# A decoder layer on one core: the next group's first norm is made inside this group's scan, in the buffer of the sums within chunks

## The chip, the core and the metric

The kernel runs on one core of a Trainium2 chip. The metric is device time in microseconds (us), the median of several executions. One more execution was recorded by the hardware profiler; every duration of a single instruction below comes from that execution, whose own time is told apart from the median.

The engines are named as the profile names them: PE multiplies matrices (and transposes, by a product with a unit matrix), PEld loads its weights, DVE works on vectors, ACT applies functions and copies, POOL is the general engine, SP issues most of the transfers. Each runs its own list of instructions in order, and they meet in semaphores.

## What is computed

One decoder layer over 64 sequences of 128 tokens with 256 features, all in float32. In short:

```
xn = layernorm(x) * gamma + beta                  # the first norm
x_inner, z = split(xn @ W_in)                     # 256 -> 2 x 512
xc = silu(conv4(x_inner) + b)                     # causal, 4 taps, per channel
B, C, delta = split(xc @ W_x)                     # 16, 16, 1
y = selective_scan(xc, A, B, C, softplus(delta))  # h = exp(dt*A)*h + dt*B*x ; y = C.h
x1 = layernorm(x + x + ((y + xc * D) * silu(z)) @ W_out)
x2 = layernorm(x1 + decayed_attention(x1, context))
out = layernorm(x2 + shared_ffn(x2) + sum of the best 2 of 8 routed ffns, weighted)
```

The scan is not run step by step. Its decay is the same for all channels, so it becomes products: within a sequence of 128 tokens, pairs of tokens in different chunks of 16 are coupled by a product of `cj` and `bj` on PE, pairs in the same chunk by elementwise sums (the "sums within chunks", tile `eq`), and both together make the 128 x 128 matrix `mt` that multiplies the scaled inputs `xd`.

## The kernel before, in words

The 64 sequences are 16 groups of 4. Each group goes through a first half (`front`, L632, then `scan`, L750), a second half (`after`, L824: output projection, norm, attention, norm; then `route`, L946: router, ranks, scatter of the rows to a buffer in DRAM) and a shared feed-forward network (`early_shared`, L1069). After 4, 8, 12 and 16 groups a batch of tiles of routed rows is listed, and the tiles' feed-forward networks (`one_tile`, L1284) run beside the later groups and, after all groups, alone. At the end the rows come back, are added, normalised and stored.

These strands are Python generators. Each `yield` says how long, in the builder's own books (`work[0]`), the strand should let others put work on PE before it goes on. `abreast` (L1312) always advances the able strand with the smallest due time, and `placed` (L1330) gives a strand its due time from the work and waits it has passed. So the order of PE's list is fixed while the program is built; after that, each of the other engines' lists is put in order by the scheduler of the framework, which may move an instruction ahead of ones that were written before it.

`first_halves` (L1500) takes group 0 and then groups 2 to 15; group 1 has a strand and buffers of its own.

The steps that the change and the prediction touch, in their order within a first half:

- `front` takes the buffer `xn` (one slot, tag "xn"), calls `layernorm` (L577) for groups other than 0, waits 2.6 in the books, transposes `xn` on PE into `xnT` (L548, L606), waits 1.2, and projects with `w_in_s`: four products with a convolution after each (L657, L662), four for the gate `sz` (L674). Then the projection with `w_x_s` and its copy `bcs` (L687), whose rows go through DRAM and come back as `bj`, `cj` and `cq` (L692 to L719, all issued by SP), a transposition of `bcs` (L695), and a chain of small operations on DVE and ACT that makes the step size `dl` (L726 to L747).
- `layernorm` issues, for 4 sequences, 4 bn_stats and 4 bn_aggr on DVE (L583, L584), an addition (L586), a power on POOL (`rstd`, L588), a product on DVE (`shift`, L590), yields 4.2 in the books, and then 4 activations on ACT that write the normalised rows (L593).
- `scan` multiplies `bj` and `cj` by masks on POOL (L754), spreads `dl` (`d1`, `dlb`, L757, L761), sums it with products (`after_in`, L764; `middle`, L773), takes the buffer `eq` under the tag "xn", which is the slot that `xn` had (L765), takes exponentials on ACT (L778, L779), multiplies `bj` and `cj` (L780, L781), multiplies `cj` by `bj` on PE (L785), and makes the sums within chunks on DVE (L788, L789, `gq` L793, then `mt` L795, L799). Then four blocks of `xc` are transposed and copied by ACT to `xd` (L806, L807), and four times four products `mt` by `xd` (L813) are combined on DVE (L817, L820).

The one slot that the change uses twice, and the wait in the books that it touches:

```
def buffer(st, shape, name, tag=None):
    if "own" not in st:
        return one.tile(shape, F32, name=name, tag=tag or name)
...
        xn = buffer(st, [P, GB, D], "xn", "xn")
...
        eq = buffer(st, [P, GB, NS, Q], "eq", "xn")
```

A new tile of a tag with one slot may be written only when the readers of the tile before it in that slot are done.

Of the kernel before, what the change touches and what calls it, by code (L numbers as in the profile page):

```python
# [16 lines left out]
P = 128  # L17
L = 128
D = 256
# [10 lines left out]
GB = 4  # L30
# [481 lines left out]
def _shared_decay(ctx, K):  # L512
    tc, nc = K.tc, K.tc.nc
    NG = K.x.shape[0] // GB
# [32 lines left out]
    def turn(out, src, ident):  # L547
        work[0] += 0.11  # L548
        nc.tensor.transpose(out, src, ident)  # L549
# [4 lines left out]
# [4 lines that stand above are left out]
        return shaped(st["own"][tag or name], shape)  # L558

    def little(st, shape, name, bufs=1):  # L560
        if "own" not in st:
            return small.tile(shape, F32, name=name, bufs=bufs)
        size = int(np.prod(shape[1:]))
        rest = st["own"]["little"]
        st["own"]["little"] = rest[:, size:]
        return shaped(rest, shape)

    def shaped(flat, shape):
        names = "abc"[: len(shape) - 1]
        sizes = dict(zip(names, shape[1:]))  # L570
        return flat[:, 0 : int(np.prod(shape[1:]))].rearrange(
            f"p ({' '.join(names)}) -> p {' '.join(names)}", **sizes
        )
# [3 lines left out]
    def layernorm(dst, src):  # L577

        n = src.shape[1]
        mv = small.tile([P, GB, 2], F32, name="mv")[:, 0:n, :]  # L580
        for b in range(n):
            st = small.tile([P, nc.vector.BN_STATS_DIM], F32, name="st")
            nc.vector.bn_stats(st, src[:, b, :])  # L583
            nc.vector.bn_aggr(mv[:, b, :], st)  # L584
        var = small.tile([P, GB], F32, name="var")[:, 0:n]
        nc.vector.tensor_scalar(var, mv[:, :, 1], EPS, None, ALU.add)  # L586
        rstd = small.tile([P, GB], F32, name="rstd")[:, 0:n]
        nc.gpsimd.tensor_tensor(rstd, var, mhalf[:, 0:n], ALU.pow)  # L588
        shift = small.tile([P, GB], F32, name="shift")[:, 0:n]
        nc.vector.scalar_tensor_tensor(shift, mv[:, :, 0], -1.0, rstd, ALU.mult, ALU.mult)  # L590
        yield 4.2
        for b in range(n):
            nc.scalar.activation(  # L593
                dst[:, b, :], src[:, b, :], AF.Identity, bias=shift[:, b : b + 1], scale=rstd[:, b : b + 1]
            )
# [14 lines left out]
    def seqs(ap):  # L610
        return ap.rearrange("p (b l) -> p b l", l=L)
# [15 lines left out]
    def load_x(g):  # L627
        xt = xts[g % 3]
        nc.gpsimd.dma_start(out=xt, in_=x[g * GB : (g + 1) * GB].rearrange("b l d -> l b d"))
        return xt  # L630

    def front(st):  # L632


        xt = st["xt"]
        xn = buffer(st, [P, GB, D], "xn", "xn")
        if st is states[0]:
            rstd, shift = K.norm0
            for b in range(GB):
                read_by = nc.scalar.activation(  # L640
                    xn[:, b, :], xt[:, b, :], AF.Identity, bias=shift[:, b : b + 1], scale=rstd[:, b : b + 1]
                )
            first_read.append(read_by.ins.name)
        else:
            yield from layernorm(xn, xt)
        yield 2.6
        xnT = buffer(st, [P, KD, T], "xnT", "xnT")
        transposed(xnT, xn, gam, bet)
        yield 1.2
# [100 lines left out]
    def scan(st):  # L750

        xcf, dl, tok, bj, cj, cq = (st[k] for k in ("xcf", "dl", "tok", "bj", "cj", "cq"))
        for t, h in ((bj, halvesT[0]), (cj, halvesT[1])):
            nc.gpsimd.tensor_tensor(seqs(t), seqs(t), h.unsqueeze(1).to_broadcast([KB, GB, L]), ALU.mult)  # L754

        d1 = little(st, [P, GB, Q], "d1")
        nc.vector.tensor_tensor(  # L757
            d1, dl.unsqueeze(2).to_broadcast([P, GB, Q]), place.unsqueeze(1).to_broadcast([P, GB, Q]), ALU.mult
        )
        dlb = little(st, [P, GB, 32], "dlb")  # L760
        nc.vector.tensor_copy(dlb, dl.unsqueeze(2).to_broadcast([P, GB, 32]))  # L761
        yield 4.4 if fetched[0] else 2.4
        pin = pm.tile([P, GB, Q], F32, name="pm")
        product(pin.rearrange("p b i -> p (b i)"), lhsT=after_in, rhs=d1.rearrange("p b i -> p (b i)"), start=True, stop=True)  # L764
        eq = buffer(st, [P, GB, NS, Q], "eq", "xn")  # L765
        nc.vector.tensor_tensor(
            eq, pin.unsqueeze(2).to_broadcast([P, GB, NS, Q]),
            a_row.unsqueeze(1).unsqueeze(3).to_broadcast([P, GB, NS, Q]), ALU.mult,
        )
        pof = pm.tile([KB, T], F32, name="pm")  # L770
        for b in range(GB):
            for q in range(4):
                product(  # L773
                    pof[32 * q : 32 * q + 32, b * L : (b + 1) * L], lhsT=dlb[:, b, :], rhs=middle[min(q, 2)],
                    start=True, stop=True, tile_position=(0, 32 * q),
                )
        eb = buffer(st, [KB, T], "eb", "bcs")
        nc.scalar.activation(eb, pof, AF.Exp, scale=a_col)  # L778
        nc.scalar.activation(eq, eq, AF.Exp)  # L779
        nc.vector.tensor_tensor(bj, bj, eb, ALU.mult)  # L780
        nc.vector.tensor_tensor(cj, cj, eb, ALU.mult)  # L781
        yield 4.2
        pmt = pm.tile([P, GB, L], F32, name="pm")
        for b in range(GB):
            product(  # L785
                pmt[:, b, :], lhsT=bj[:, b * L : (b + 1) * L], rhs=cj[:, b * L : (b + 1) * L], start=True, stop=True
            )
        nc.vector.tensor_tensor(eq, eq, cq, ALU.mult)  # L788
        nc.vector.tensor_tensor(  # L789
            eq, eq, tok[:, :, 0:NS].unsqueeze(3).to_broadcast([P, GB, NS, Q]), ALU.mult  # L790
        )
        gq = little(st, [P, GB, Q], "gq")
        nc.vector.tensor_reduce(gq, eq.rearrange("p b n i -> p b i n"), AX.X, ALU.add)  # L793
        mt = buffer(st, [P, GB, NQ, Q], "mt", "dm")
        nc.vector.tensor_tensor(  # L795
            mt, gq.unsqueeze(2).to_broadcast([P, GB, NQ, Q]), causal.unsqueeze(1).to_broadcast([P, GB, NQ, Q]), ALU.mult
        )
        mtf = mt.rearrange("p b j i -> p b (j i)")
        nc.vector.tensor_tensor(mtf, mtf, pmt, ALU.add)  # L799
        yield  # L800

        xd = [buffer(st, [P, 2, DI], f"xd{j}", tag) for j, tag in enumerate(("xnT", "xd"))]
        for b in range(GB):
            ps = pm.tile([P, DI], F32, name="pm")
            for c in range(CI):
                turn(ps[:, c * P : (c + 1) * P], xcf[:, c, b * L : (b + 1) * L], ident)  # L806
            nc.scalar.activation(xd[b // 2][:, b % 2, :], ps, AF.Copy, scale=dl[:, b : b + 1])  # L807
            yield 0.5 if b < GB - 1 else 3.6
        acc = st["sz"]
        for c in range(CI):  # L810
            ps = pm.tile([P, GB, L], F32, name="pm")
            for b in range(GB):
                product(  # L813
                    ps[:, b, :], lhsT=xd[b // 2][:, b % 2, c * P : (c + 1) * P], rhs=mtf[:, b, :], start=True, stop=True
                )
            y = xcf[:, c, :]
            nc.vector.scalar_tensor_tensor(  # L817
                y, xcf[:, c, :], dsk[:, c : c + 1], ps.rearrange("p b l -> p (b l)"), ALU.mult, ALU.add
            )
            nc.vector.tensor_tensor(acc[:, c, :], acc[:, c, :], y, ALU.mult)  # L820
            yield 0.5 if c < CI - 1 or not fetched[0] else 2.0
        st["acc"] = acc
# [507 lines left out]
    def placed(gen, at, length, span=1.0):  # L1330

        passed = 0.0
        while True:
            before = work[0]
            try:
                wait = next(gen) or 0.0
            except StopIteration:
                return
            passed += work[0] - before + wait
            yield at + span * min(1.0, passed / length), wait  # L1340
# [15 lines left out]
    states = [{} for _ in range(NG)]  # L1356
# [142 lines left out]

    def first_halves():  # L1500
        states[2]["xt"] = load_x(2)
        yield from placed(start, 0.0, 54.0)
        states[0]["scanned"] = True
        for g in range(2, NG):
            if g + 1 < NG:
                yield from until(lambda: "read" in states[g - 2], g - 1)
                states[g + 1]["xt"] = load_x(g + 1)
            yield from placed(first_half(states[g]), g - 1, 54.0)
            states[g]["scanned"] = True
# [327 lines left out]
```

## Time and profile before

| | |
|---|---|
| median of 3 executions | 1954.57 us (1946.59 to 1956.8) |
| the profiled execution, its own time | 1935.52 us |
| its span, first to last instruction | 1933.7 us |
| mean granted clock of PE | 0.988 |
| busy: PE, DVE, ACT, POOL | 97%, 50%, 39%, 24% |
| PE idle, by stretch: 0 to 80 us | 21.8 us |
| 80 to 400 us | 16.5 us |
| 400 to 1450 us | 11.2 us |
| 1450 to the end | 18.1 us |

The idle time of a stretch is its length less PE's busy time in the table of stretches. PE's busy time is counted with modelled ends, so a PE that is shown busy may still have short pauses. A row of a wait names the engine that waited, the line and tile it waited with, who released it, the total, the number of waits and the longest.

### The profile page before, as it was taken

The page shows a single profiled execution, that of the slowest core. Times are in us where ns is not written, and L with a number is a line of the kernel's source. Part 1 is how long each engine was busy: PE and PEld are TensorE (multiplying, and loading weights), DVE is VectorE, ACT ScalarE, POOL GpSimd, SP SyncE. Part 2 cuts the span into 40 slices and gives each one's busy share as a digit, 9 for nine tenths or more (in the row PEclk, how much of TensorE's full clock was granted, in tenths as well). Part 3 has the DMA queues.
Part 4 walks back from the last instruction along what each step waited for, and adds up shares of the span by engine and source line. Part 5 has one row for each costly group of instructions (what it writes and reads, how often), then busy time and mean ns, then how long its engine had stood idle before and what let it go on. Part 6 is the DMA issues. An engine that isn't in the chain of part 4 may idle for free.

```text
span 1933.7 us, 26599 instructions
## 1 busy us (share of the span) xinstructions
PE 1866.0 (97%) x9252; PEld 1393.1 (72%) x9252; DVE 971.9 (50%) x2409; ACT 748.7 (39%) x1238; POOL 473.1 (24%) x715
## 2 busy tenths in 40 slices
PE   7799999999999998999999999999999999999997
PEld 3656656668686856787877768786877888999554
DVE  5766667745455557455555474554333111111774
ACT  5553553443434343535353544352231222222233
POOL 2102212303030403132322313141313322222111
PEclk9999999999999998999999999999999999999998
DMA  4211211423150214323242224232204443353782
GB/s 142 53 35 44 68 49 41 137 85 95 45 153 28 85 35 153 101 77 113 64 133 93 79 93 123 61 123 92 81 19 128 146 150 118 120 175 107 276 305 89
DMA packets 101352, 199.10 MB, mean 103 GB/s; under 512 B 22904, under 2 KB 61432, under 8 KB 96600
## 3 DMA queue, kind: packets, MB, share of 16 engines
q1 hardware_dynamic: 80952, 144.24, 23.6%
q0 software_dynamic: 17328, 51.41, 7.8%
q10 hardware_dynamic: 2928, 1.65, 0.3%
q8 instruction: 75, 1.23, 0.3%
q14 instruction: 69, 0.57, 0.1%
HBM read 206.81 MB, written 58.08 MB: 137 GB/s over the span
## 4 chain that ended last, share of the span: by engine, by line
PE 72%; DVE 3%; issue 3%; DMA 2%; ACT 2%; POOL 2%; SPq 0%; POOLq 0%; ACTq 0%; DVEq 0%
PE pm L545 37%; PE gu L545 32%; PE pm L549 4%; DMA picked<-ys 1%; POOL rstd L588 1%; DMA ys<-rows_out,to 1%; DVE st L583 0%; DVE x L1305 0%; DMA cq<-chunks 0%; POOL xs L1028 0%; ACT x L593 0%; ACT xn L593 0%; DVE hc L1051 0%; DVE xt L1305 0%; ACT xc L667 0%
## 5 line engine op out<-in xcount | busy, mean ns | idle before, releaser
L545 PE MATMUL gu<-rows_T,routed_gu 128*128 128x256 f32 (+1 forms) x2496 | 499.4, 351 | 1.5 <-ACT rows_T L1232 1.5
L545 PEld LDWEIGHTS gu<-rows_T,routed_gu 128*128 128x128 f32 x2496 | 417.7, 191 | 59.2 <-issue 14.2
L1261 DVE TENSOR_TENSOR hid<-hid,gu 128x512 f32<-128x512 f32 x135 | 92.7, 687 | 394.8 <-PE gu L545 344.4
L545 PE MATMUL pm<-routed_d,hid 128*128 128x256 f32 x1080 | 252.7, 381 | 0.0
L545 PE MATMUL gu<-x2T,shared_w 128*128 128x512 f32 x512 | 232.0, 596 | 4.4 <-DVE hc L1051 3.3
L545 PE MATMUL pm<-xnT,w_in_s 128*128 128x512 f32 x480 | 226.6, 599 | 1.7 <-ACT xnT L606 1.1
L545 PEld LDWEIGHTS pm<-routed_d,hid 128*128 128x128 f32 x1080 | 199.7, 190 | 29.6 <-issue 5.4
L1277 POOL DMA_INDIRECT ys<-rows_out,to x135 | 135.0, 1000 | 331.4 <-ACT rows_out L1276 282.8
L545 PEld LDWEIGHTS gu<-x2T,shared_w 128*128 128x128 f32 x512 | 94.3, 190 | 112.1 <-issue 93.6
L593 ACT ACTIVATE x<-x,shift,rstd 128x256 f32<-128x256 f32 x156 | 82.3, 590 | 232.5 <-DVE shift L590 222.2
L588 POOL TENSOR_TENSOR rstd<-var,mhalf 128x4 f32<-128x4 f32 (+1 forms) x69 | 72.8, 1055 | 370.6 <-DVE var L586 318.6
L662 DVE SCALAR_TENSOR_TENSOR xc<-pm,cw,xc 128x508 f32<-128x508 f32 (+1 forms) x180 | 131.4, 738 | 37.2 <-ACT xc L657 36.0
L545 PEld LDWEIGHTS pm<-xnT,w_in_s 128*128 128x128 f32 x480 | 90.2, 192 | 80.3 <-issue 72.3
L1276 ACT ACTIVATE rows_out<-pm,wt 128x256 f32<-128x256 f32 x135 | 57.9, 471 | 205.2 <-PE pm L545 185.4
L1260 ACT ACTIVATE hid<-gu 128x512 f32<-128x512 f32 x135 | 80.6, 597 | 110.0 <-PE gu L545 109.7
L545 PE MATMUL pm<-w_out_s,sz 128*128 128x256 f32 x512 | 116.4, 381 | 0.4 <-ACT xd L807 0.2
L545 PEld LDWEIGHTS pm<-w_out_s,sz 128*128 128x128 f32 x512 | 95.4, 191 | 14.3 <-issue 1.0
L657 ACT ACTIVATE xc<-pm,cb,cw 128x512 f32<-128x512 f32 x60 | 46.7, 778 | 144.2 <-PE pm L545 144.2
L1028 POOL DMA_INDIRECT xs<-x,index x64 | 71.6, 1118 | 78.0 <-DVE row L1024 42.8
L583 DVE BATCH_NORM_STATS2 st<-x 128x6 f32<-128x256 f32 x196 | 77.4, 408 | 1.6 <-DMA x<-in_x_dram 0.7
L545 PE MATMUL gu<-shared_w,hc 128*128 128x256 f32 x320 | 72.5, 380 | 0.0
L1051 DVE TENSOR_TENSOR hc<-hc,gu 128x512 f32<-128x512 f32 x64 | 43.5, 680 | 55.2 <-PE gu L545 35.1
(288 smaller groups left out, 2571.2 us busy)
## 6 DMA issues: line engine op xcount, KB each, us to landing
routed_gu<-in_ffn_dram SPq DMA_DIRECT2D x78, 1024.0 KB
routed_d<-in_ffn_dram SPq DMA_DIRECT2D x78, 512.0 KB
picked<-ys SPq DMA_DIRECT2D x16, 1024.0 KB
rows_in<-xs SPq DMA_DIRECT2D x57, 258.0 KB
cT<-in_ctxT_dram POOLq DMA_DIRECT2D x16, 512.0 KB, 4.1
x_rows<-x SPq DMA_DIRECT2D x16, 512.0 KB
cq<-chunks SPq DMA_DIRECT2D x15, 512.0 KB
x<-in_x_dram POOLq DMA_DIRECT2D x9, 512.0 KB, 4.2
```

The costliest lines, as they stand in the source:

```text
L545: nc.tensor.matmul(out, lhsT=lhsT, rhs=rhs, **how)
L549: nc.tensor.transpose(out, src, ident)
L583: nc.vector.bn_stats(st, src[:, b, :])
L588: nc.gpsimd.tensor_tensor(rstd, var, mhalf[:, 0:n], ALU.pow)
L593: nc.scalar.activation(dst[:, b, :], src[:, b, :], AF.Identity, bias=shift[:, b : b + 1], scale=rstd[:, b : b + 1])
L657: nc.scalar.activation(xcf[:, c, :], ps, AF.Identity, bias=cb[:, c : c + 1], scale=cw[:, c, TAPS - 1 : TAPS],)
L662: nc.vector.scalar_tensor_tensor(xc[:, c, :, s:], ps3[:, :, : L - s], cw[:, c, TAPS - 1 - s : TAPS - s], xc[:, c, :, s:], ALU.mult, ALU.add,)
L1028: s = nc.gpsimd.indirect_dma_start(out=xs, in_=rows[k][:, b, :], in_offset=None, out_offset=bass.IndirectOffsetOnAxis(ap=index[:, b, k : k ...
L1260: nc.scalar.activation(hc, psg, AF.Silu)
L1261: nc.vector.tensor_tensor(hc, hc, psu, ALU.mult)
L1276: nc.scalar.activation(y[:, j, :], ps[:, j, :], AF.Copy, scale=wt[:, j : j + 1])
L1277: s = nc.gpsimd.indirect_dma_start(out=ys, in_=y[:, j, :], in_offset=None, out_offset=bass.IndirectOffsetOnAxis(ap=to[:, j : j + 1], axis=0),)
```

## The change

The scan of a group whose successor's input is there now ends its sums within chunks by taking the slot "xn" again, for the next group's `xn`, and starts the next group's `layernorm` (the part ahead of its yield). The second part, the four activations, is written after the last `xd`. The next group's `front` finds `xn` made and skips the norm and the wait of 2.6. This is so for the norms of groups 2 to 15, made in the scans of group 0 and of groups 2 to 14; groups 0 and 1 are as before.

```diff
@@ front
         xt = st["xt"]
-        xn = buffer(st, [P, GB, D], "xn", "xn")
-        if st is states[0]:
+        made = "xn" in st
+        if made:
+            xn = st["xn"]
+        else:
+            xn = buffer(st, [P, GB, D], "xn", "xn")
+        if made:
+            pass
+        elif st is states[0]:
...
         else:
             yield from layernorm(xn, xt)
-        yield 2.6
+        yield 0.0 if made else 2.6
@@ scan, after mt is made
         nc.vector.tensor_tensor(mtf, mtf, pmt, ALU.add)
+
+        norm = None
+        if "next" in st:
+            then = st["next"]
+            xn = then["xn"] = buffer(then, [P, GB, D], "xn", "xn")
+            norm = layernorm(xn, then["xt"])
+            next(norm)
         yield
@@ scan, after the last xd
+        for _ in norm or ():
+            pass
@@ first_halves
         states[2]["xt"] = load_x(2)
+        for g in (0, *range(2, NG - 1)):
+            states[g]["next"] = states[max(g + 1, 2)]
```

Lines of the kernel after the change stand 6 lower from the transposition in `front` on, 13 lower at `xd` and 15 lower behind it.

## The prediction

> **What bounds the kernel now.** First the page's head: is one engine the bound, and where does it pause?
>
> ```profile
> span 1933.7 us, 26599 instructions
> ...
> PE 1866.0 (97%) x9252; PEld 1393.1 (72%) x9252; DVE 971.9 (50%) x2409; ACT 748.7 (39%) x1238; POOL 473.1 (24%) x715
> ...
> PE   7799999999999998999999999999999999999997
> ...
> PEclk9999999999999998999999999999999999999998
> ```
>
> PE is the bound. The change leaves its products as they are, so it can only move PE's pauses, 67.7 us in all (1933.7 less 1866.0), and the clock. The table of stretches says where the pauses are: 21.8 us before 80, 16.5 from 80 to 400, 11.2 from 400 to 1450, 18.1 after. The built order of PE's list is the same up to group 2's norm, and the last stretch has no first halves. So the question is the 28 us in between. PE's waits from 80 to 400 us name them:
>
> ```profile
> engine line waited for: us in total, times, longest us
> PE pm L549 <- ACT xn L593: 8.7, 9, 2.0
> PE pm L545 <- DVE sel L985: 2.8, 1, 2.8
> PE pm L545 <- DVE mt L799: 1.6, 2, 0.8
> PE gu L545 <- ACT rows_T L1232: 0.7, 1, 0.7
> PE pm L545 <- ACT x2T L604: 0.7, 1, 0.7
> ```
>
> The first row is the target: the transposition of `xn` waits for the norm at the starts of groups 2 to 6, before routed tiles fill the gaps. After 400 us it is nothing (8.8 us in the whole run, group 0 apart). The stretches around three of these waits (after the two times: PE, PEld, DVE, ACT, POOL busy, then the granted clock):
>
> ```profile
> 93.00:96.00 3.00, 0.98 (x9) 0.79 (x8) 2.10 (x6) 1.41 (x4) 1.38 (x1) 1.00 0.00 0
> 96.00:100.00 4.00, 4.00 (x17) 3.05 (x16) 2.23 (x4) 2.39 (x4) 0.00 (x0) 0.57 0.00 0
> 311.00:314.00 3.00, 1.36 (x5) 0.35 (x4) 0.52 (x4) 1.22 (x3) 1.01 (x1) 1.00 0.00 0
> 314.00:317.00 3.00, 3.00 (x13) 1.76 (x14) 0.34 (x1) 2.75 (x5) 0.00 (x0) 1.00 0.03 8
> 386.00:389.00 3.00, 0.85 (x5) 0.53 (x5) 0.26 (x2) 1.52 (x4) 1.39 (x4) 1.00 0.97 402
> 389.00:394.00 5.00, 5.00 (x13) 2.57 (x12) 0.69 (x1) 2.00 (x4) 0.00 (x0) 0.66 0.79 308
> ```
>
> A pause of about 2 us (first and third) is followed by a low clock, 0.57 over 4 us and 0.66 over 5 us, which costs 1.7 us each; 1.6 us (second) is not.
>
> **What it removes.** (a) The xn waits, 8.7. (b) Two low clocks behind them, 3.4. (c) In group 2's stretch the order changes, so the `sel` wait there (2.8) goes, with the low clock behind it (0.60 from 142 to 149 us, 2.8). (d) The `mt` waits of groups 3 and 4, 1.6, counted anew under (f), and `rows_T`, 0.7, which gets 3.4 us of products ahead of it. Sum 20.0.
>
> **What it adds: cover.** With the norm gone, a group's chain after `bcs` starts earlier and stands elsewhere in PE's list. I compare the PE work between two steps of the chain with the time that the chain took in the trace (transposed `bcs` to `dlb` 6.0 us in four groups of five; `middle` to `cj` 4.5 to 4.7; `cj` to `mt` 7.2 to 7.4). Work is counted in the built order at 0.86 us for a product of 512 columns, 0.43 for 256, 0.22 for 128, 0.11 for a transposition (the trace has 3.6 us for 8 records of 512 and for 16 of 256, two records to a product, and 1.04 for 8 transpositions).
>
> ```
>               bcs to dlb      middle to cj    cj to mt
> needed        6.0             4.6             7.3
> group         before  after   before  after   before  after
> 2             4.2     0.2     8.9     4.1     2.8     7.1
> 3, 4          6.6     6.9     4.4     5.2     6.1     7.1
> 5             6.6     6.9     4.4     5.2     6.1     3.7
> 9             0.6     7.6     1.0     1.0     6.1     2.6
> others        >10     >10      >6      >5.3     >9      >11
> ```
>
> (e) Group 2: in the changed order `bcs` is followed at once by `after_in`, with nothing between. The scheduler has also drawn the next norm's DVE part ahead of the scan's sums, to between `tok` and `dlb`: 4 bn_stats at 0.41, 4 bn_aggr at 0.17, two at 0.16, and about 0.94 of waiting for POOL's power (`shift` waited 61.7 us in 66 times), 3.6 us, in front of the rest of that chain. So the pause is 6.0 + 3.6 less 0.2, 9.3 us; without the norm in the way it would be 5.8, and if both norms' waits add up, 11. I take 9.3, less 0.2 that it waited before: 9.1. A low clock after it costs 1.7 for one window or 3.4 for two; 2.5. Then `cj` 0.5, and `sel` 1.4, since the DVE reaches the router's `pb` only after `gq`. Sum 13.5.
>
> (f) Groups 3, 4, 5: a new wait on ACT. `xn` lies in the slot of `eq`, so the four activations must wait for the reduce `gq`. In the built order of ACT they stand after the first `xd`, ahead of three others, which PE needs for all its `mt` products. The trace of group 3 now:
>
> ```profile
> 215.18 1.13 PE L545 MATMUL pm<-cj,bj 128*128 128x128 f32 x8
> 216.08 1.23 DVE L788 TENSOR_TENSOR eq<-eq,cq 128x1024 f32<-128x1024 f32 x1 [1.05 <-DMA cq<-chunks]
> 217.39 2.42 ACT L807 ACTIVATE xd<-pm,dl 128x512 f32<-128x512 f32 x4 [1.11 <-DVE eq L788]
> 219.08 1.88 DVE L793 TENSOR_REDUCE gq<-eq 128x64 f32<-128x1024 f32 x1
> 222.67 1.58 PE L545 MATMUL pm<-mt,xd 128*128 128x128 f32 x12 [0.82 <-DVE mt L799]
> ```
>
> All four `xd` were done 1.2 us before `gq`. Now three come after it: `gq` ends about 5.4 us after `cj`, then 2.35 for four activations (590 ns each), then 1.8, so the last `xd` is there at 9.8 against products due at 7.1 to 7.8. Part of that runs under the products of the first rows: 2.1 us each in groups 3 and 4; between 0.3 (if `gq` is early) and 3. In group 5 only 3.7 us of work stand before `mt`, and `sel` stands in front of `xc`: 5.2 us. Low clocks: 1.7 in group 5, 1.0 in groups 3 and 4 together (each about even). Sum 12.1.
>
> (g) Smaller: the router's first product now comes straight behind the transposition, 0.7 three times (the `x2T` row); `w_in` straight behind it in group 6, 0.9 and 0.3 elsewhere; `qh` in groups 4 and 5 has 3.5 instead of 4.3 us of cover, 0.5 each. Sum 4.3, between 1 and 6.
>
> (h) Group 9 (725 to 736 us), where no tiles are listed, waits 8.0 us now. Afterwards 7.6 us stand behind `bcs`, so that wait ends, but `cj` is 3.1 us too early (4.1 in the trace less 1.0) and `mt` 4.6: 7.7 in two pieces. With a shorter low clock (0.54 from 727 to 742 us now) minus 1.5, between minus 4 and plus 1.
>
> (i) POOL's power is moved ahead of the masks of `bj` and `cj`, in group 2 behind the one of `bj`, which waits for a transfer; 1.0 us each under PE's work. The norm issues no transfers. The other groups keep more cover than needed: nothing, unless the second rival holds.
>
> Here a rule speaks against the change. The Trainium skill (TensorE: Matmul & The Clock Gate, HAM oscillation) says that PE must not idle for more than about 3.4 us. By it the xn waits, 2.2 us at most, never cost clock, and the 9 us pause in group 2 does: the removed 6.2 (b and c) fall out, and 4.2 (group 2, group 5) stay added. By the rows 6.2 go and 5.2 come. I follow the rows; the rule would make the sum 5 us worse.
>
> **Sum.** 13.5 + 12.1 + 4.3 less 1.5 less 20.0 is 8.4 us slower, on a profiled execution of 1935.5 us (span 1933.7, 1.8 around it): 1943.9, times 1.0043. The median is 1954.57, 1% above that execution; by the same ratio, 1963.
>
> **Rivals.** Within 0.5% (1944.8 to 1964.3) a measurement can't tell it from no change.
>
> *It does what it says and the new waits are covered.* `gq` is early, `xd` isn't held, the norm's DVE part falls into DVE's own waits. Then (f) is 0, (e) is 5.8 + 1.7 + 1.4, with (g) 13.2, less 21.5: 8 us faster, 1946, from 1938 to 1952. For it: DVE is 50% busy, ACT 39%. Against: four groups' covers are within 1 us of the need.
>
> *ACT held in the later groups.* In groups 6 to 14 `xn` stands in ACT's list, waiting for `gq`, ahead of other `xd` and of the tiles' activations (`hid`, L1260), which empty the three banks of `gu`. It decides from the point where ACT is late by more than the banks hold, about 5 us (three times 1.7). Price: 2.35 plus a wait of up to 1, of which I let 1.7 through in nine groups: 15 more, 23 slower, 1978, from 1966 to 1995. For it: those `xd` have ACT rows that wait for PE, not the other way, so nothing there is tried yet. Against: cover of 12 us for a need of 7 to 10.
>
> *Nothing moves*, because the scheduler's order absorbs it: 1954.6.
>
> **Chances.** Likeliest case 0.47, own range 1955 to 1972 (0.27 within, 0.20 slower); covered 0.18 (0.10 faster, 0.08 within); ACT held 0.30, all slower; nothing 0.05, within. Faster 0.10, same 0.40, slower 0.50. Range 1944 to 1982: it leaves out a third of the covered case and the far end of the held one.
>
> **What would show it.** Right: the xn row gone from PE's waits; one wait of 8 to 10 us on `dlb` near 120 us with a low clock behind; `xd` rows of ACT that wait for `xn` or `gq`, and PE waiting 2 us for `xd` three times before 400 us; group 9 waiting on `mt`. Wrong: PE idle from 80 to 400 us under 12 us (covered), or waits on `hid` and `xd` after 400 us (ACT held).

## The result, and the profile after

The changed kernel takes 1974.74 us (median of 4 runs, 1972.06 to 1980.06) where the kernel before took 1955.68 (4 runs, 1946.59 to 1958.89). The measured ratio is 1.0133, 95% interval 1.0110 to 1.0155: 1.3% slower, or 26 us on 1955. The ratios here and below are of fast runs alone; one of the 22 runs of `e1_xnT_first`, 2198 us at a granted clock of 0.845, is left out.

The two medians alone are only 19 us apart (1.0097), which lies below that interval; why the two differ is not known. The run `e4_early` below, which has most of the change, was compared with 44 runs of the kernel before, and there the medians and the ratio agree (1.0126 and 1.0125, 24 us). The profiled execution took 1973.7 us.

The page's head answers to the one of before. PE's idle time is the span less its busy time: 97.0 us, where it was 67.7. The busy time rose by 9.0 for the same 9252 instructions. About 6 of these are low clock, since the mean granted clock fell from 0.988 to 0.985 (0.3% of 1972 us); what the other 3 are is not known.

```profile
span 1972.0 us, 26615 instructions
...
PE 1875.0 (95%) x9252; PEld 1394.2 (71%) x9252; DVE 992.2 (50%) x2409; ACT 754.7 (38%) x1245; POOL 470.6 (24%) x715
...
PE   7879899989999998999999999999999999999997
...
PEclk9889999999999999999999999999999999999999
```

Idle time in the same stretches of the two traces:

| stretch | before | after |
|---|---|---|
| 0 to 80 us | 21.8 | 21.7 |
| 80 to 480 us | 16.5 | 36.5 |
| 480 to 800 us | 8.2 | 11.1 |
| 800 to 1450 us | 3.1 | 5.3 |
| 1450 us to the end | 18.1 | 22.5 |

Most of the loss is where the routed tiles do not yet fill PE. PE's waits from 80 to 480 us name it (total, times, longest):

```profile
PE pm L545 <- ACT xnT L606: 18.4, 4, 5.3
PE pm L545 <- DVE dlb L767: 9.9, 1, 9.9
PE pm L545 <- DVE mk L1019: 5.1, 3, 4.0
PE pm L545 <- ACT x2T L604: 1.3, 4, 0.4
```

The row of `xn` is gone, as the change intends. Its place is taken by the first product of `w_in`, which waits for `xnT`, the copy of the transposed norm, in groups 3 to 6. The prediction gave this row 1.2 us (0.9 and 0.3 in its sum). The second row is the pause of group 2 that it had foreseen (9.3, measured 9.9). Here is group 3's start, in order of time (start, duration, and in brackets the idle time before it and who ended it):

```profile
157.00 0.17 DVE L586 TENSOR_SCALAR var<-mv 128x4 f32<-128x4 f32 x1
158.51 1.04 PE L549 MATMUL pm<-ident,xn 128*128 128x128 f32 x8
159.44 0.96 POOL L1043 DMA_INDIRECT xs<-row,index  x1 [0.30 <-issue]
160.41 0.81 POOL L629 DMA_DIRECT2D x<-in_x_dram  x1
161.24 1.07 POOL L588 TENSOR_TENSOR rstd<-var,mhalf 128x4 f32<-128x4 f32 x1
162.34 0.16 DVE L590 SCALAR_TENSOR_TENSOR shift<-mv,rstd 128x4 f32<-128x4 f32 x1 [4.58 <-POOL rstd L588]
162.54 1.58 ACT L593 ACTIVATE x<-x,shift,rstd 128x256 f32<-128x256 f32 x3 [16.42 <-DVE shift L590]
164.03 1.42 ACT L606 ACTIVATE xnT<-pm,bet,gam 128x512 f32<-128x512 f32 x2
164.84 2.07 PE L545 MATMUL pm<-xnT,w_in_s 128*128 128x512 f32 x2 [4.43 <-ACT xnT L606]
```

Read it from the bottom. PE waits 4.43 us for `xnT`. ACT could have made it from 159.5 on, when the transposition was done, but three activations of another strand stand ahead of it: those of `x1`, group 1's second norm. They wait for `shift`, which waits for the power `rstd` on POOL. Its input `var` had been ready at 157.2, but POOL worked through the last three of eight scatters of the rows of group 0 (0.96 us each and 0.30 between them) and a load. So a wait of POOL's list reaches PE through three other lists. The clock after the four pauses (columns as in the prediction):

```profile
164.80:168.80 4.00, 3.96 (x8) 2.10 (x9) 1.39 (x3) 1.65 (x3) 0.00 (x0) 0.63 0.00 0
245.90:250.00 4.10, 4.09 (x7) 2.03 (x8) 0.89 (x2) 1.70 (x3) 0.00 (x0) 0.58 0.00 0
323.40:327.40 4.00, 3.98 (x5) 1.83 (x6) 0.90 (x2) 1.29 (x3) 0.00 (x0) 0.50 0.00 0
403.20:407.20 4.00, 4.00 (x7) 1.87 (x8) 0.86 (x2) 1.39 (x3) 0.32 (x2) 0.57 0.89 276
```

In groups 3 to 6 it is 0.63, 0.58, 0.50 and 0.57 over about 4 us: 6.9 us more. Waits and clock make 25.3 us.

In the kernel before this did not happen. The `front` had 4.2 and 2.6 in the books ahead of the transposition, in which PE got other work, and in group 3 `x1`'s four activations began at 162.20, 5.7 us ahead of the transposition of `xn`:

```profile
162.20 2.08 ACT L593 ACTIVATE x<-x,shift,rstd 128x256 f32<-128x256 f32 x4 [13.76 <-DVE shift L590]
167.89 0.33 PE L549 MATMUL pm<-ident,xn 128*128 128x128 f32 x1 [1.07 <-ACT xn L593]
```

The change took away not only a norm but also this distance; the third set of runs below puts it back.

### The profile page after: what moved, and what is told of

The parts are those of the page before. It is cut to its first block, busy times and chain, and to the rows that moved or that the text cites. A ratio compares the mean times of both kernels' runs of the same rounds, so it can differ in the third digit from the quotient of the medians.

```text
span 1972.0 us, 26615 instructions
## 1 busy us (share of the span) xinstructions
PE 1875.0 (95%) x9252; PEld 1394.2 (71%) x9252; DVE 992.2 (50%) x2409; ACT 754.7 (38%) x1245; POOL 470.6 (24%) x715
## 3 DMA queue, kind: packets, MB, share of 16 engines
q8 instruction: 75, 1.23, 0.3%
## 5 line engine op out<-in xcount | busy, mean ns | idle before, releaser
L545 PE MATMUL pm<-xnT,w_in_s 128*128 128x512 f32 x480 | 234.4, 614 | 20.2 <-ACT xnT L606 19.1
L1043 POOL DMA_INDIRECT xs<-x,index x64 | 65.9, 1030 | 159.2 <-issue 74.4
L1247 ACT COPY rows_T<-pm 128x512 f32<-128x512 f32 (+1 forms) x78 | 40.9, 526 | 93.6 <-PE pm L549 86.3
```

The source lines that it names most:

```text
L545: nc.tensor.matmul(out, lhsT=lhsT, rhs=rhs, **how)
L1043: s = nc.gpsimd.indirect_dma_start(out=xs, in_=rows[k][:, b, :], in_offset=None, out_offset=bass.IndirectOffsetOnAxis(ap=index[:, b, k : k ...
L1247: nc.scalar.copy(tT, ps)
```

## The experiments

**Theory 1**: the loss is the order of ACT's list; `xnT` stands behind `x1`'s activations, and these behind POOL's scatters. **Theory 2** is the prediction's step (f): `xn`'s activations wait for `gq`, since they use its slot, and hold three `xd`. **Theory 3** is the rival: ACT is held in the later groups. The chips differed (the kernel before had medians of 1934 to 1956 us in these sessions), so only ratios to it are compared; the last column puts the ratio on 1955 us.

| run | ratio | 95% interval | us |
|---|---|---|---|
| the change | 1.0133 | 1.0110 to 1.0155 | +26.0 |
| e1_xnT_first | 0.9985 | 0.9976 to 0.9993 | -2.9 |
| e2_scatters_later | 1.0040 | 1.0026 to 1.0054 | +7.8 |
| e4_early | 1.0125 | 1.0109 to 1.0142 | +24.4 |
| e4_late | 0.9981 | 0.9972 to 0.9991 | -3.7 |
| f1_xn_behind_xd | 0.9987 | 0.9979 to 0.9995 | -2.5 |
| f2_stay | 1.0041 | 1.0029 to 1.0054 | +8.0 |
| f3_not_group2 | 0.9970 | 0.9958 to 0.9981 | -5.9 |
| f5_late | 0.9967 | 0.9954 to 0.9980 | -6.5 |
| g_wait26 | 1.0081 | 1.0062 to 1.0100 | +15.8 |
| g_wait68 | 1.0005 | 0.9997 to 1.0012 | +1.0 |
| g_rank | 0.9965 | 0.9952 to 0.9978 | -6.8 |
| h_wait68_early | 0.9958 | 0.9943 to 0.9973 | -8.2 |

**First set: where the loss is, and by which list.** In `e1_xnT_first` each of `x1`'s activations gets a dependency, of order only, on the newest copy of `xnT`:

```diff
@@ layernorm, its four activations; behind is the list of xnT copies for x1, else empty
+            for name in behind[-1:]:
+                tc.add_manual_dep(
+                    a.ins, name, mybir.DependencyInfo(mybir.DependencyClass.NoSync, mybir.DependencyReason.SCHED_ONLY),
+                    reason="order of the list",
+                )
```

> The changed kernel, with one edit of order on ACT: the four activations of the second half's first norm (x1) stand behind the newest copies of xnT instead of three of them ahead. PE's list is the same, no operation is added. Theory 1 (xnT stands behind x1's activations, which wait for POOL): the four waits of PE for xnT, 18.4 us between 80 and 480 us, fall to about 1 us each, and the low clocks behind them (0.63, 0.58, 0.50, 0.57 over 4 us each: 6.9 us) go: 22 us less than the changed kernel, about 1953, within 0.5% of the kernel before; up to 8 us of it may come back as waits of PE for x1T or for banks, since x1's activations then stand ahead of the convolution's copies. Theory 2 (the loss is the slot: xn's activations wait for gq ahead of xd): nothing moves, 1972 to 1977. Theory 3 (the loss is group 2's pause and the later groups): nothing moves either.

The ratio falls from 1.0133 to 0.9985, 29 us where 22 were expected, with the same operations and an edit that orders ACT's list alone. The row of `xnT` from 80 to 480 us falls from 18.4 to 0.5 us. In its trace `xnT` no longer waits for POOL, and `x1` comes as late as it did:

```profile
157.36 1.45 ACT L613 ACTIVATE xnT<-pm,bet,gam 128x512 f32<-128x512 f32 x2 [13.02 <-PE pm L549]
159.44 1.07 POOL L590 TENSOR_TENSOR rstd<-var,mhalf 128x4 f32<-128x4 f32 x1
160.73 2.08 ACT L595 ACTIVATE x<-x,shift,rstd 128x256 f32<-128x256 f32 x4 [1.93 <-DVE shift L592]
```

PE is busy without a gap from 153 to 165 us there, at full clock: nothing came back behind `x1`. The edit takes back the whole loss and 3 us more, so Theory 1 holds for all of it.

In `e2_scatters_later` ACT's order stays wrong, and the scatters of a group are written behind the next group's `x1` power on POOL (not where a batch of tiles follows, so group 6 keeps its scatters ahead):

```diff
@@ route; scatter(k) issues what the loop over b did
+            if late_one:
+                scatters.append((scatter, k))
+            else:
+                scatter(k)
             yield 5.0
@@ after; each scatter is ordered behind the power of x1 and the load of cT
         left = next(norm) + work[0]
+        while scatters:
+            scatter, k = scatters.pop(0)
+            scatter(k, (powers[-1], brought.ins.name))
```

> The changed kernel, with the eight indirect scatters of a group's rows put behind the power (rstd) of the next group's x1 norm in POOL's list, in all groups after which no batch of tiles is listed. ACT's and PE's lists are left as they are, x1's activations still stand ahead of xnT. Theory 1 in its full form (x1's activations wait because the power stands behind scatters of about 1.3 us each): rstd follows var by about 1.5 us instead of 4.2, so the xnT waits of groups 3 to 5 fall from 4.4 to 1 to 2 us each and most of their low clocks go: 10 to 15 us less than the changed kernel, 1960 to 1965; group 6 (scatters of group 4's rows not moved) keeps its 5.3 us. If the power's place does not matter (x1's rows themselves are late): no change, 1972 to 1977. If the moved scatters hold something else on POOL (the masks of bj and cj, the load of cT): slower than 1980.

18 us of the 26 go, slightly more than expected. The power follows its input at once, and only group 6 (5.2 us) still waits for `xnT`:

```profile
158.42 0.17 DVE L588 TENSOR_SCALAR var<-mv 128x4 f32<-128x4 f32 x1
158.68 1.03 POOL L590 TENSOR_TENSOR rstd<-var,mhalf 128x4 f32<-128x4 f32 x1 [0.19 <-DVE var L588]
```

```profile
PE pm L545 <- ACT xnT L608: 6.4, 4, 5.2
```

So both links are needed: the scatters make the power late, and ACT's order lets that reach PE. Mending ACT's order takes back the whole loss, mending POOL's takes it back where it was tried.

`e4_early` and `e4_late` restrict the loop in `first_halves` to the scans `(0, 2, 3, 4, 5)` and `range(6, NG - 1)`.

> The changed kernel with the early norm only for groups 2 to 6; from group 7 on as before. Theory 1 (loss of about 23 us in groups 2 to 6, about 5 in groups 7 to 9, 4 gained in group 9, nothing after): within 5 us of the changed kernel, 1970 to 1978. Rival (ACT held by xn in the later groups): about 1955 to 1962.

> The changed kernel with the early norm only for groups 7 to 15; groups 2 to 6 as before. Theory 1: within 0.3% of the kernel before, 1952 to 1960. Rival (ACT held by xn in the later groups): 12 us or more above the kernel before, 1967 to 1975.

All of the loss is in groups 2 to 6 (1.0125); in groups 7 to 15 the early norm gains a little (0.9981). Theory 3 falls.

**Second set: the other steps, with `xnT` first.** Each is the first run with one more edit:

```diff
@@ scan, f1_xn_behind_xd: xn's activations behind the last xd
+            norm = layernorm(xn, then["xt"], last)
...
+        last.append(scaled.ins.name)
@@ scan, f2_stay: bn_stats behind the last addition to mt
+            norm = layernorm(xn, then["xt"], stats_behind=[summed_mt.ins.name])
@@ first_halves, f3_not_group2
-        for g in (0, *range(2, NG - 1)):
+        for g in range(2, NG - 1):
```

`f1_xn_behind_xd` adds the same kind of dependency from `xn`'s activations to the last `xd`; `f2_stay` from the next norm's `bn_stats` to the last addition to `mt` on DVE; `f3_not_group2` leaves 0 out of the loop in `first_halves`; `f5_late` is `e4_late` with `xnT` first.

> As the first run (xnT ahead of x1's activations), and on ACT the four activations of the next group's xn stand behind the fourth xd copy of the scan instead of ahead of three. The prediction's step (f) (xn waits for gq and so holds three xd, 12.1 us with its low clocks in groups 3 to 5): 8 to 12 us less than the first run, ratio to before 0.992 to 0.995. The reading of the trace after (PE never waits for xd there; the 4.1 us before group 5's router product are DVE's, whose rank stands behind gq): nothing, ratio 0.998 to 0.9995, and the 4.1 us stay.

0.9987 against 0.9985: nothing. Step (f) held no PE at all; theory 2 falls. The trace after shows why in group 3. The three late `xd` stand behind `xn`, as predicted, but PE still has 12 transpositions to do, and its first product `mt` by `xd` follows without a wait:

```profile
222.87 2.08 ACT L593 ACTIVATE xn<-x,shift,rstd 128x256 f32<-128x256 f32 x4 [0.56 <-DVE gq L799]
224.16 1.51 PE L549 MATMUL pm<-ident,xc 128*128 128x128 f32 x12
224.85 1.82 ACT L820 ACTIVATE xd<-pm,dl 128x512 f32<-128x512 f32 x3
225.51 0.39 PE L545 MATMUL pm<-mt,xd 128*128 128x128 f32 x2
```

The wait that the prediction put there in group 5 is another one. There DVE does the router's `rank` only behind the scan's `gq`, and PE waits for the selection (`sel`, `mk`) while `xn` runs beside it:

```profile
376.31 1.85 DVE L799 TENSOR_REDUCE gq<-eq 128x64 f32<-128x1024 f32 x1
378.08 0.41 DVE L998 TENSOR_REDUCE rank<-gt 128x32 f32<-128x256 f32 x1
378.25 2.08 ACT L593 ACTIVATE xn<-x,shift,rstd 128x256 f32<-128x256 f32 x4 [2.89 <-DVE gq L799]
379.01 0.17 DVE L1000 TENSOR_SCALAR sel<-rank 128x32 f32<-128x32 f32 x1
379.33 0.55 PE L545 MATMUL pm<-sel,upto 128*128 128x32 f32 x2 [3.97 <-DVE mk L1019]
```

> As the first run, and on DVE the next norm's statistics (bn_stats) stand behind the last addition to mt, where the source writes them, in every group, instead of ahead of the scan's sums. The prediction's step (e) (3.6 us of the pause of 10 us in group 2 are the hoisted norm): the pause falls to 6 to 6.5 us, and the ratio to before to 0.996 to 0.997. If the pause is set by the chain from bcs to dlb alone: it stays above 9 us and the ratio at 0.9985. If the later norm then makes xn late: new waits for xn on PE in groups 3 to 6, ratio above 1.

A miss. The pause stays at 9.0 us (10.0 in the first run), so the hoisted norm was worth 1 us of it, not 3.6. And the kernel gets 11 us slower than the first run. Its waits show 4.2 of these:

```profile
PE pm L545 <- DVE dlb L780: 9.0, 1, 9.0
PE pm L545 <- DVE kh L889: 4.2, 3, 1.6
```

With the statistics behind `mt`, the second half's rotation `kh` is late, a row that the first run does not have here. The rest of the 11 is not assigned. The scheduler's hoist was the better order. What stands in the pause in its trace is the end of the second half on the same engines: the norm of `x2` on DVE, and on ACT `x2`'s first activation (0.60 us) ahead of the table load (1.28) and the logarithm that `dl` waits for. No run took these away, so that they set the pause is a reading of the trace.

> As the first run, and group 2's own norm is made as before the change (group 0's scan makes none). By the prediction's steps (c) and (e): the pause on dlb (10 us and 1.8 of low clock) goes, the wait for xn (2.2 and 1.7) and the wait for sel (2.9 and 2.8) of the kernel before come back: 2 us less than the first run, ratio 0.997 to 0.998. If the order behind bcs is not what opened the pause: it stays, and the wait for xn comes on top, 4 us more, ratio 1.0005.

0.997, as expected within its interval. The pause on `dlb` goes, `xn` (2.0 us) and `sel` (4.0) are waited for again.

> As the first run, with the early norm only for groups 7 to 15. Against the run with late groups alone (0.998) this tells what xnT behind x1's activations costs beside routed tiles: the waits for xnT in the late groups were 4.5 us in all, so 2 to 4 us less, 0.996 to 0.997; if they are covered, 0.998. Against the first run it tells what the early norm is worth in groups 2 to 6 when the order on ACT is mended: waits for xn, 8.7 and two low clocks against group 2's pause and its clock, 11.8: about even.

0.9967, about even with f3; against `e4_late` (0.9981) the intervals overlap, so what `xnT`'s place costs beside the tiles is not told apart from nothing. Against the first run (0.9985) it is 3.5 us less, with intervals that touch: with ACT's order mended and the wait in the books still gone, the early norm in groups 2 to 6 brings no gain.

**Third set: the place in the books, and a better kernel.** Two runs keep a wait ahead of the transposition, though `xn` is made; a third orders the scan's sums behind the router's `sel` on DVE, on top of f3.

```diff
@@ front, g_wait26
-        yield 0.0 if made else 2.6
+        yield 2.6
@@ front, g_wait68
-        yield 0.0 if made else 2.6
+        yield 6.8 if made else 2.6
@@ scan, g_rank
-        nc.vector.tensor_tensor(eq, eq, cq, ALU.mult)
+        scaled_eq = nc.vector.tensor_tensor(eq, eq, cq, ALU.mult)
+        for name in selected_by[-1:]:
+            ordered(scaled_eq, name)
```

> The changed kernel, with the wait of 2.6 in the books kept ahead of the transposition of xn although xn is made. ACT's order is not touched by hand. If the xnT waits come from the transposition being put too early against x1's norm: 2.6 us of other products go ahead of it each time, so each of the four waits (4.4, 4.4, 4.4, 5.3 us) falls to about 2 us and some low clocks go: 10 to 14 us less than the changed kernel, ratio to before 1.006 to 1.008. If only ACT's order counts: no change, 1.0133.

1.0081, at the edge of what was expected: the `xnT` row falls from 18.4 to 3.9 us, but the chains behind it get other covers (`dlb` 5.9 in three waits).

> The changed kernel, with 6.8 in the books ahead of the transposition of xn, which is what the norm (4.2) and the wait behind it (2.6) took there before: the norm is early, the front stands where it stood. If the whole loss is the earlier place of the front (xnT ahead of x1's norm, nothing between bcs and after_in in group 2): both go, and the waits for xn (8.7 us and 3.4 of low clock) stay away: ratio 0.994 to 0.996. If the early norm costs by itself (its statistics in DVE's chain, xn on ACT ahead of xd): 0.999 to 1.004.

1.0005: a number of the second case, but not for its reason. From 80 to 480 us the run did what the first case expected: PE is idle 11.7 us there, 16.5 in the kernel before. Behind that, one wait takes it back:

```profile
PE pm L545 <- DVE dlb L767: 11.6, 5, 9.6
```

```profile
721.54 0.17 DVE L1016 COPY x<-slot 128x4 f32<-128x4 f32 x1 [4.21 <-DMA x_rows<-x]
```

In group 9, where no tile is listed, DVE stands 4.2 us at a copy of the second half into rows that a transfer still reads, ahead of the chain to `dlb`. The last run shows that this order comes with the early norms of the later groups.

> As the third run of the second set (xnT first, group 2's norm as before), and on DVE the scan's sums within chunks stand behind the router's newest selection (sel). If the waits for sel in groups 2 and 5 (4.2 and 4.1 us, a low clock of 1.7 behind each) are DVE's order alone: they fall below 1 us, 8 to 11 us less, ratio 0.991 to 0.993. If mt then comes late by what sel came earlier: waits for mt of 2 us a group, ratio 0.997 or more.

0.9965: the row of `mk` goes and the wait for `sel` falls from 4.0 to 1.7, but 3.6 us come back in group 5, where `mt` is late (shown as `at`). The rival reading was right for that group. Against f3 (0.9970) nothing is won.

The last run takes g_wait68 with the loop of `e4_early`.

> As the run with 6.8 in the books, with the early norm only for groups 2 to 6; from group 7 on as before. In that run the first 400 us lost 11 us less than the kernel before, which the prediction's (a) and (b) put at 12.1, and groups 7 to 10 gave 9 back, 9.7 of it in one wait for dlb near 724 us. If that wait comes with the later groups' order: it falls to what it was before (3 us), and the ratio is 0.994 to 0.996, the best of all. If it comes from the first groups: it stays, and the ratio is 0.9995 to 1.001.

0.9958, 8 us under the kernel before, in its interval 5 to 11: the best of all by its middle, though g_rank, f3 and f5 overlap it. Group 9's wait is 2.8 us again, so it came with the later groups' early norms. This is the most that was got out of the change here: the row of `xn` from 80 to 480 us falls from 8.7 to 0.5, and PE is idle 11.8 us there instead of 16.5.

## Why the prediction was right or wrong

The sign was right, and 1974.7 lies in the range of 1944 to 1982. But it lies above the likeliest case's own range, 1955 to 1972, and the size was wrong: plus 8.4 forecast, plus 26.0 measured (21.5 to 30.3 by the interval of the ratio). That the sign came out is in part luck. Without step (f), whose wait is not there, the forecast would have been 3.7 us faster, and the step that cost most was put at 1.2 us.

- **(a) The `xn` row, 8.7**: gone, right.
- **(b) Two low clocks behind it, 3.4**: too much. The pause of 2.0 us near 96 us was followed by a low clock (0.50 in the stretch of 2 us that begins 2 us after it) in the trace before, but in `e4_late`, `f3_not_group2`, `f5_late` and `g_rank` the same pause of 2.0 us was followed by 1.00 throughout. The one near 388 us was followed by 0.50 in all three traces that have it. One execution's clock is not the kernel's; by these shares (1.7 for the second pause, and for the first a fifth of 1.7, one trace in five) about 2 us would have been fair. The rule of 3.4 us that the prediction set aside would have put it at nothing, which the pause near 388 us speaks against.
- **(c), (d)**: right: the wait for `sel` in group 2 and the rows of `mt` and `rows_T` are gone.
- **(e) Group 2's pause, 13.5**: 9.9 and 1.8 of low clock, 11.7. The size was near, its working was wrong (and its sum, 6.0 and 3.6 less 0.2, is 9.4 and not 9.3): `f2_stay` shows 9 us without the norm in the chain, where the prediction had 5.8. The likely reason, read from the traces: it had measured the chain where `x2`'s norm was done ahead of `bcs`, as in group 2 before (its activations end at 122.3, `bcs` begins at 122.6); after the change that norm falls into the chain.
- **(f) ACT held by `gq`, 12.1**: the three `xd` are held, but PE never waits for them (`f1_xn_behind_xd`), since its 12 transpositions cover them. A different wait, the row of `mk` of 5.1 us, 4.0 of it in group 5 with a low clock of 1.7 behind, stands at the same place. (The last `xd` was put at 9.8 us; its terms 5.4, 2.35 and 1.8 make 9.6.)
- **(g) The first `w_in` straight behind the transposition, 0.9 in group 6 and 0.3 elsewhere**: the failed step. It measured 18.4, with 6.9 of low clock, and 4.3 more in three waits from 480 to 1450 us. The runs put the loss there: `e1_xnT_first`, which changes only ACT's order, takes back 29 us. The prediction costed the copy as if ACT were free. It looked at ACT's list for `xd` and not for `xnT`, where three activations of another strand with an open wait had been put in front, and it took POOL's power as 1.0 us of work without asking what stood ahead of it on POOL.
- **(h) Group 9, minus 1.5**: the pauses there sum to 7.2 before (2.9 `dlb`, 2.3 `cj`, 1.8 `sel`, 0.3 `pre`; the prediction had 8.0) and to 5.0 after (2.3 before the product of `cj` and `bj`, 1.7 before the first of `mt`, 1.0 `pre`). So 2.2 went, about as forecast: the wait for `dlb` ended and one on `mt` came, though smaller than the 4.6 that it had.

With these sizes, read in the two traces, the sum is 11.7 + 6.8 + 25.3 + 4.3 + 0.6 (`x2T`, 1.3 less the 0.7 of before) less 2.2 and less 18.6 (a to d with 2.0 for b): 28 us, for 26 by the ratio. This agreement should not be trusted too far, since the two traces themselves differ by 38.3 us: the one of before was 1% under its median. One wait near 1508 us (3.7 us, at a product of `gu` with `rows_T`) belongs to that; waits of 2.8 to 3.8 us stand there in the traces of the first set too, and none in those of the second and third sets. What sets it was not tried, and some 7 us of the 38.3 are not assigned.

The rivals: "covered" is out (32.2 us idle from 80 to 400 us instead of under 12). "ACT held in the later groups" is out by `e4_late` (0.9981 where it had 15 us more), though its forecast of 1978 was the nearest.

## What to carry to other kernels

When a step is moved earlier, follow each thing it feeds through the list of the engine that carries it out: what stands ahead of it there, what that waits for, and what stands ahead of that on its engine. An instruction is as late as the latest open wait ahead of it in its list, even if its own inputs are there; here that made PE wait 4.4 to 5.3 us for a copy of 0.76 us. And a wait in the books that is removed with the step may have kept two strands apart. Keep the distance first and shorten it by trial: here 6.8, 2.6 and 0 in the books gave ratios of 1.0005, 1.0081 and 1.0133.

## What the runs showed of the hardware

A short DVE instruction can be stretched to the end of a POOL instruction. In the trace of `f2_stay` a product of 128x4 numbers, which takes 0.16 us elsewhere, takes 0.94 and ends with POOL's mask of `bj`, at 129.95 and 129.93 us:

```profile
128.66 1.27 POOL L773 TENSOR_TENSOR bj<-bj,halfT 128x512 f32<-128x512 f32 x1 [2.03 <-DMA bj<-rows]
129.01 0.94 DVE L762 TENSOR_TENSOR lg<-lg,dd 128x4 f32<-128x4 f32 x1 [1.29 <-ACT lg L753]
```

The product `d` (128x64) shows the same in the trace after. It took 0.22 or 0.23 us ten times, and 1.23 to 1.34 us the five times that it began within 0.13 us behind the start of POOL's mask of `cj`. Where it began 0.05 us ahead of that mask, at 209.60, it took 0.22 and the mask 1.30 instead of 1.27. The Trainium skill (SBUF — State Buffer, SBUF: two separate sides) has this as an exclusive lock: a DVE operation with two inputs in SBUF and a POOL operation that reads SBUF share a port pair, and the second waits for the first. The times agree with it. In the pause of group 2 in `f2_stay` it stretches `lg` by 0.8 us and `d` by 1.0.
